# Four conv layers on one core: first loads and setup in steps, ln and exp in pieces, last sums ahead of the last products

## The chip, the cores and the metric

The kernel runs on one core of one Trainium2 chip. The core has a matmul engine (TensorE, PE in the profile, with its weight loads as PEld), a vector engine (VectorE, DVE), a scalar engine for activations (ScalarE, ACT), GpSimd (POOL) and a queue engine (SyncE, SP) that mostly issues DMAs. ACT and POOL issue DMAs too. SBUF is the on-chip memory of 128 partitions, PSUM the memory that PE writes. The metric is the device time in microseconds (us) of one execution, as the median of several runs.

## The reference, cut to what matters

Four layers act on x of shape (4, 64, 64, 64): four images of 4096 pixels with 64 channels, all float32.

```
# layer 0: attention over the pixels of each image
q = x @ Wq + bq ; k = x @ Wk + bk ; v = x @ Wv + bv
x = gamma * transposed_softmax_product(softmax(q k^T), v) + x   # einsum('bmn,bmc->bnc', attn, v)
# layer 1: a convolution block
y = pw1(layernorm(x)) ; y = depthwise3x3(y) ; y = y1 * y2 ; y = y * pw_sca(mean(y)) ; x = x + pw2(y) * beta
z = pw3(layernorm(x)) ; z = z1 * z2 ; x = x + pw4(z) * gamma
# layer 2: attention without weights, on x read as (B, C, H, W)
x = softmax(xf^T xf) applied to xf, + x
# layer 3: attention with 32 inner channels, then a normalisation over all images
f = softmax(theta(x) phi(x)^T) ; y = f g(x) ; w = y @ w_W + w_b
x = x + (gamma * (w - mean(w)) / sqrt(var(w) + 1e-3) + beta)     # mean and var over images and pixels
```

## The kernel before

**The work.** Each image's x lies in SBUF as `X[:, b]`: two halves of 64 partitions (the channels, for two groups of columns), 2048 numbers each. An attention layer is a loop over items. An item makes score tiles on PE into PSUM, ACT takes the exponential of each tile into an `e` buffer, and a later step multiplies these by the values, into an accumulator. PSUM has three score tiles of 1024 columns (`ps`, `new_ps`) and two accumulators of 512 (`acc`, `new_acc`); a new one takes over the oldest and waits until that is read. There are six `e` buffers and a ring of two `t` buffers (`new_t`), used in the same way.

**Layer 0** (L1018) has 32 items per image, each of four score tiles (L1031, exponential L1036), with products at L1056 that DVE adds up at L1063. `project0` (L971) makes the query and value projections of an image. For image 0 the queries come in four steps, with a bias add on DVE (L1002); for images 1 to 3 they come in two steps named "once" (L982), with two bias adds on DVE (L990) and a DMA on SP for each (L993) that copies the half to the other partitions. bq enters as `bqk`, a product of the folded weights with bq (`fold_qk`, L859 to 877).

**Layer 1** (L1112) is a generator of small steps, most of them on DVE (convolution taps L1157), some on PE and ACT, which runs under the items of layers 0 and 2. `setup` (L879) turns the small vectors of all layers into columns (`vec`), folds layer-norm scales and shifts into the weights `pw1` and `pw3` and their biases `pwb`, and builds the constants `half` and `resb`, which later steps use.

**Layer 2** (L1231) has 32 items per image, each of four score tiles (L1245, exponential L1253); products (L1262) come one item later. `close2` (L1289) scales and adds the result into x on DVE; `open3` (L1305) then makes theta, phi and g for layer 3 (L1315, L1325, L1340, with bias adds on DVE).

**Layer 3** (L1349) has two blocks of 32 items per image. An item makes two score tiles (L1361) and two exponentials (L1367) into one `e`; products (L1389) come two items later. The softmax's sums are collected in two ways: for every tenth item PE multiplies `e` by ones (L1378) into a second accumulator z; all others are added on DVE into `esum` (L1385), which `sums` (L1397) multiplies by ones at the block's end. When a block is done, ACT copies the product out (`yz`, L1395), `totals` (L1404) calls `sums`, takes 1/z as exp(-ln z) on ACT (L1410, L1411), improves it by a Newton step on DVE (L1412, L1413) and scales yz (L1414), and `close` (L1424) projects the block, adds a bias on ACT (L1432) and takes statistics on DVE. The last block of the last image ends in `close_last` (L1436).

**The order.** PE, ACT and DVE run in the order in which the program issues; a planner within the program sets it. `run` (L1495) first issues the start by hand: weights folded, half of image 0's x turned (`load_x`, L920), the query bias, the first query step, the second half of x. Then it goes through the items. After an item's scores, and again after the steps registered for that item by `at(i, fn)`, two lanes (`conv`, `misc`) tick by the item's number of microseconds; a generator in a lane runs its next step when the number that it last yielded has passed. So the numbers in `yield` are an order, not times. DMAs on SP, ACT and POOL go in the order of the program: x of image 0 is issued on SP and ACT (`fetch_x`, L738), then on SP bq, gamma, the small vectors (`rows`) and the x of images 1 to 3; the remaining weights are on POOL, behind the identity matrix.

**Layers in sequence**: layer 0 for images 0 to 3; layer 2 for image 0 and 1, layer 3 for image 0, layer 2 for image 2, layer 3 for image 1, layer 2 for image 3, layer 3 for images 2 and 3. So layer 2 of images 2 and 3 follows directly on a layer 3, and only layer 3 of image 3 follows on another layer 3.

**The end.** `finish` (L1536) combines the statistics and writes eight halves of images: three through PSUM (L1566, DVE L1585, stores L1575), five by an add on DVE (L1600), a turn on PE (L1607), a copy (L1627; L1630 and L1631 for the last), and a store of 512 KB (L1579). `check_sums` (L1635) counts values out of range into `bad`, which every engine reads before it ends.

Of the kernel before, what the change touches and what calls it, by code (L numbers as in the profile page):

```python
# [691 lines left out]
def fast_path(ctx: ExitStack, tc: tile.TileContext, a: dict, out: bass.AP, bad):  # L692
# [44 lines left out]

    def fetch_x(b, queues):  # L738
        if b % 2 == 0:
            fetch_x.both = new_big("xr")  # L740
        t = fetch_x.both[:, bass.ts(b % 2, 2048)].rearrange("p (q n) -> p q n", n=128)
        src = a["x"][b].rearrange(by_rows, p=2, q=16)
        for g in range(2):
            for p in range(2):
                (queues[p] if b == 0 else queues[g]).dma_start(
                    out=t[64 * p : 64 * p + 64, bass.ts(g, 8)], in_=src[p, :, bass.ts(g, 8)]
                )
        rows_x.append(t)
# [3 lines left out]
    nc.sync.dma_start(out=qk[:, 64:128], in_=a["L0_conv_Wk"])  # L752
    fetch_x(0, (nc.sync, nc.scalar))
    bq = const.tile([64, 1], F32, name="bq")
    nc.sync.dma_start(out=bq, in_=a["L0_conv_bq"].rearrange("(n o) -> n o", o=1))
# [123 lines left out]
    def setup():  # L879
# [7 lines left out]
        for i, (w_, sh, bi) in enumerate(  # L887
            ((pw1, "L1_conv_ln1_b", "L1_conv_pw1_b"), (pw3, "L1_conv_ln2_b", "L1_conv_pw3_b"))
        ):
            for r in range(2):  # L890
                mm(
                    ps[:, 2 * i + r : 2 * i + r + 1], w_[0:64, bass.ts(r, 128)], V(sh, 0, 0, 64),
                    start=True, stop=True,
                )
            nc.vector.tensor_add(
                pwb[:, i, :], ps[:, 2 * i : 2 * i + 2], vec[:, col[bi] : col[bi] + 2]
            )

        ps = new_ps()
        for i, (w_, g) in enumerate(((pw1, "L1_conv_ln1_g"), (pw3, "L1_conv_ln2_g"))):  # L900
            nc.vector.tensor_scalar_mul(w_, w_, V(g))
            mm(ps[:, 512 * i : 512 * i + 256], cmat, w_, start=True, stop=True)
            nc.vector.tensor_copy(w_, ps[:, 512 * i : 512 * i + 256])
        for i in range(4):
            nc.vector.tensor_scalar_mul(half[:, bass.ts(i, 64)], ident[:, 0:64], 0.5)
            stt(
                half[:, bass.ts(i, 64)], ident[:, 64:128], -0.5 if i > 1 else 0.5,
                half[:, bass.ts(i, 64)], ALU.mult, ALU.add,
            )
        nc.vector.tensor_mul(resb[:, 0:1], V("L1_conv_pw2_b"), V("L1_conv_beta"))  # L910
        nc.vector.tensor_mul(resb[:, 1:2], V("L1_conv_pw4_b"), V("L1_conv_gamma"))
        yield 3.0
# [7 lines left out]
    def load_x(b):  # L920
        for g in range(2):
            ps = new_ps()
            for i in range(8):
                nc.tensor.transpose(ps[:, bass.ts(i, 128)], rows_x[b][:, 8 * g + i, :], ident)
            (nc.vector.tensor_copy if g else nc.scalar.copy)(X[:, b, bass.ts(g, 1024)], ps)
            yield 3.0
# [44 lines left out]
    def project0(b):  # L971
# [5 lines left out]
        for j, w in once if b else ((0, "q"), (0, "v"), (1, "q"), (2, "q"), (1, "v"), (3, "q")):  # L977
            ps = new_ps()
            if w == "once":
# [7 lines left out]
                for o in range(2):  # L987
                    own, other = slice(64 * o, 64 * o + 64), slice(64 - 64 * o, 128 - 64 * o)
                    n = bass.ts(2 * j + o, 512)
                    nc.vector.tensor_scalar_add(  # L990
                        qs[own, :, n], ps[own, :].rearrange("p (s n) -> p s n", s=2), bqk[own, :]
# [25 lines left out]

    def layer0(b):  # L1018
# [3 lines left out]
        def scores(t):  # L1022
# [3 lines left out]
            for g in range(4):  # L1026
                ps = new_ps()
# [203 lines left out]
    def layer2(b):  # L1231
# [51 lines left out]
        for n in range(32):  # L1283
            items.append((lambda n=n: scores(n), 4.6))
            at(first + n + 1, lambda n=n: products(n))
# [3 lines left out]
    def close2(b):  # L1289
# [4 lines left out]
        for i in range(4):  # L1294
# [4 lines left out]
            yield 2.0 if i < 3 else 6.0  # L1299
# [3 lines left out]
    wys, early = {}, []  # L1303

# [44 lines left out]
    def layer3(b):  # L1349
# [3 lines left out]
        def scores(n):  # L1353
# [12 lines left out]
            for kp in range(2):  # L1366
                act(e[:, bass.ts(kp, 1024)], tiles[kp], AF.Exp)  # L1367

        def products(n):
# [4 lines left out]
            if mc % 10 == 9 or (last and n >= 62):  # L1374
# [9 lines left out]
            elif mc:  # L1384
                nc.vector.tensor_add(esum, esum, e)  # L1385
            if last and n == 63:
                sums()
            for k in range(4):
                mm(  # L1389
                    st["y"][32 * k : 32 * k + 32, :], m.gx[:, mc, :], e[:, bass.ts(k, 512)],  # L1390
                    start=mc == 0, stop=mc == 31,
                )
            if mc == 31 and not (last and n == 63):
                st["yz"] = new_t("yz")
                nc.scalar.copy(st["yz"][:, 0:512], st["y"])  # L1395

# [7 lines left out]
        def totals(nb):  # L1404
            sums()
            yz, z = st["yz"], st["z"]

            t = new_t("inv")
            r, d = t[:, 0:512], t[:, 512:1024]
            act(r, z, AF.Ln)  # L1410
            act(r, r, AF.Exp, scale=-1.0)  # L1411
            nc.vector.tensor_mul(d, z, r)  # L1412
            stt(d, d, -2.0, r, ALU.add, ALU.mult, accum_out=inv3[:, 2 * b + nb : 2 * b + nb + 1])  # L1413
            stt(yz[:, 0:512], d, -1.0, yz[:, 0:512], ALU.mult, ALU.mult)  # L1414

# [42 lines left out]
        for n in range(64):  # L1458
# [4 lines left out]
            elif n % 32 == 31:  # L1463
                at(first + n + (2 if n == 63 and b < 2 else 4), lambda n=n: totals(n // 32))
                at(first + n + 8, lambda n=n: close(n // 32))
# [29 lines left out]
    def run():  # L1495
# [6 lines left out]
        next(loads)  # L1502
        misc.add(first)
# [32 lines left out]
    def finish():  # L1536
# [34 lines left out]
        def store(i, o):  # L1571
            dst = out[i // 2].rearrange(by_rows, p=2, q=16)[:, :, bass.ts(i % 2, 8)]
            if i < E:
                for p in range(2):
                    nc.sync.dma_start(  # L1575
                        out=dst[p].rearrange("h q n -> h (q n)"), in_=o[64 * p : 64 * p + 64, 0:1024]
                    )
            else:
                nc.sync.dma_start(out=dst.rearrange("p h q n -> h p (q n)"), in_=o[:, 0:1024])  # L1579
# [42 lines left out]
        for i in range(E, 2 * B):  # L1622
# [5 lines left out]
            else:  # L1628
                check_sums(mv)
                nc.vector.tensor_copy(os[i][:, 0:512], pss[i][:, 0:512])  # L1630
                nc.scalar.copy(os[i][:, 512:1024], pss[i][:, 512:1024])  # L1631
            store(i, os[i])
# [74 lines left out]
```

## Time and profile before

| | |
|---|---|
| median of 3 runs | 2654.57 us (2653.53 to 2654.67) |
| profiled execution, its own time | 2654.59 us |
| its span, first to last instruction | 2652.8 us |
| PE, DVE, ACT, POOL busy | 2612.8, 1348.6, 1718.6, 16.4 us |
| mean granted PE clock | 0.997 |
| score matmul groups L1031, L1245, L1361 on PE | 475.5, 469.8, 309.5 us |
| product groups L1056, L1262, L1389 on PE | 467.4, 468.5, 272.0 us |
| exponentials L1036, L1253, L1367 on ACT | 517.1, 517.0, 496.0 us |
| esum adds L1385 on DVE, one | 2.29 us |

A line of the timeline gives the start and length of a group of instructions in us, engine, source line, operation, output and input, the count, and in brackets how long the engine was idle just before and what ended that. A line of waits gives the waiting engine and line, what it waited for, the total in us, how often, and the longest. A line of a table of windows gives the window, its length, the busy us and count of PE, PEld, DVE, ACT and POOL, the granted PE clock, the share of time in which the DMA engines were busy, and GB/s.

### The profile page before, as it was taken

The numbers are of one execution on the slowest core, as the hardware profiler recorded it, in microseconds if no ns is written. First come the engines' busy times: TensorE is split into PE (matmuls) and PEld (weight loads), VectorE is DVE, ScalarE is ACT, GpSimd is POOL, SyncE is SP. The second block draws the span as 40 slices with busy tenths as digits, with TensorE's granted clock in tenths as the row PEclk, the third lists the DMA queues.
The fourth block names the chain that finished last, engine by engine and source line by source line (L and its number), as shares of the span: only waits on it lengthen the run. The fifth ranks groups of instructions, "written<-read, shape, count | busy, mean of one in ns | idle before, by whom it ended". The sixth has DMA issues, their size and how long they took to land.

```text
span 2652.8 us, 50797 instructions
## 1 busy us (share of the span) xinstructions
PE 2612.8 (98%) x22421; PEld 830.2 (31%) x22421; DVE 1348.6 (51%) x1555; ACT 1718.6 (65%) x2787; POOL 16.4 (1%) x66
## 2 busy tenths in 40 slices
PE   8999999999999999999999999999999999999998
PEld 3333233333323323333333322243322333322223
DVE  3232386633876338621672148800068600098997
ACT  4555655656566565666656668756578755578886
POOL 2000000000000000000000000000000000000000
PEclk9999999999999999999999999999999999999999
DMA  3000000001000100010010000010000010010002
GB/s 73 1 17 1 17 8 10 1 17 25 9 1 1 32 17 1 1 33 17 1 33 17 17 1 1 2 33 1 17 1 2 1 33 1 1 33 2 1 1 66
DMA packets 24282, 36.46 MB, mean 14 GB/s; under 512 B 3725, under 2 KB 12150, under 8 KB 24054
## 3 DMA queue, kind: packets, MB, share of 16 engines
q1 hardware_dynamic: 23141, 32.03, 5.5%
q8 instruction: 178, 2.92, 0.5%
q0 software_dynamic: 672, 0.56, 0.1%
q10 hardware_dynamic: 240, 0.54, 0.1%
q14 instruction: 51, 0.41, 0.1%
HBM read 4.80 MB, written 4.19 MB: 3 GB/s over the span
## 4 chain that ended last, share of the span: by engine, by line
PE 93%; DVE 4%; ACT 2%; issue 0%; DMA 0%; SPq 0%; DVEq 0%; ACTq 0%
PE acc L1056 17%; PE acc L1262 17%; PE ps L1031 17%; PE ps L1245 16%; PE ps L1361 10%; PE acc L1389 8%; PE ps L1118 2%; DVE tg L1385 2%; PE accz L1378 1%; ACT e L1253 1%; PE ps L1209 1%; PE ps L1186 1%; PE ps L1088 1%; PE ps L1340 1%; PE ps L1007 0%
## 5 line engine op out<-in xcount | busy, mean ns | idle before, releaser
L1036 ACT ACTIVATE e<-ps 128x1024 f32<-128x1024 f32 x512 | 517.1, 1025 | 338.1 <-PE ps L1031 225.8
L1253 ACT ACTIVATE e<-ps 128x1024 f32<-128x1024 f32 x512 | 517.0, 1025 | 305.0 <-PE ps L1245 304.9
L1367 ACT ACTIVATE e<-ps 128x1024 f32<-128x1024 f32 x512 | 496.0, 1022 | 85.4 <-PE ps L1361 78.3
L1385 DVE TENSOR_TENSOR tg<-tg,e 128x2048 f32<-128x2048 f32 x214 | 490.4, 2292 | 24.7 <-ACT e L1367 5.7
L1031 PE MATMUL ps<-X,q 64*64 64x512 f32 x4096 | 475.5, 599 | 7.6 <-DVE q L990 4.1
L1245 PE MATMUL ps<-ko 64*64 64x512 f32 x4096 | 469.8, 591 | 2.2 <-ACT ko L1227 1.6
L1262 PE MATMUL acc<-e,X 64*64 64x512 f32 x4096 | 468.5, 591 | 2.6 <-DVE inv L1412 1.6
L1056 PE MATMUL acc<-e,vq 128*64 128x512 f32 x2048 | 467.4, 598 | 0.0
L1063 DVE SCALAR_TENSOR_TENSOR yv<-acc,gam,yv 128x512 f32<-128x512 f32 x224 | 167.8, 750 | 322.6 <-PE acc L1056 311.7
L1157 DVE SCALAR_TENSOR_TENSOR y<-pad,vec,y 128x1024 f32<-128x1024 f32 x240 | 308.1, 1284 | 8.1 <-ACT pad L1141 1.0
L1361 PE MATMUL ps<-tg,ph 32*64 32x512 f32 x4096 | 309.5, 613 | 1.4 <-DVE tg L1329 0.5
L1389 PE MATMUL acc<-e,tg 128*32 128x512 f32 x2048 | 272.0, 603 | 1.5 <-ACT yz L1395 1.5
L1245 PEld LDWEIGHTS ps<-ko 64*64 64x64 f32 x4096 | 157.7, 132 | 288.1 <-issue 195.4
L1262 PEld LDWEIGHTS acc<-e,X 64*64 64x64 f32 x4096 | 159.1, 133 | 278.7 <-issue 263.3
L1031 PEld LDWEIGHTS ps<-X,q 64*64 64x64 f32 x4096 | 143.2, 133 | 323.7 <-issue 224.8
L1056 PEld LDWEIGHTS acc<-e,vq 128*64 128x64 f32 x2048 | 136.0, 136 | 315.1 <-issue 294.4
L1270 DVE TENSOR_TENSOR ph<-ph,acc 128x512 f32<-128x512 f32 x16 | 11.0, 688 | 379.6 <-ACT ph L1269 379.6
L1361 PEld LDWEIGHTS ps<-tg,ph 32*64 32x64 f32 x4096 | 79.5, 129 | 218.7 <-issue 143.2
L1389 PEld LDWEIGHTS acc<-e,tg 128*32 128x32 f32 x2048 | 43.5, 108 | 202.3 <-issue 196.3
L1253 ACT ACTIVATION_READ_ACCUMULATOR e<-ps 128x1 f32 x512 | 106.1, 207 | 0.0
L1036 ACT ACTIVATION_READ_ACCUMULATOR e<-ps 128x1 f32 x512 | 106.0, 207 | 0.0
L1141 ACT ACTIVATE pad<-ps,pwb 128x512 f32<-128x512 f32 x64 | 44.6, 697 | 45.7 <-PE ps L1118 39.0
(193 smaller groups left out, 939.9 us busy)
## 6 DMA issues: line engine op xcount, KB each, us to landing
xn<-t SPq DMA_DIRECT2D x64, 128.0 KB
ph<-tg SPq DMA_DIRECT2D x64, 128.0 KB
ko<-ko SPq DMA_DIRECT2D x16, 256.0 KB
xr<-in_x_dram SPq DMA_DIRECT2D x14, 256.0 KB
q<-q SPq DMA_DIRECT2D x12, 256.0 KB
out_dram<-o SPq DMA_DIRECT2D x5, 512.0 KB
out_dram<-o SPq DMA_DIRECT2D x6, 256.0 KB
xr<-in_x_dram ACTq DMA_DIRECT2D x2, 256.0 KB
```

The lines of the kernel that those rows point to most:

```text
L1031: mm(ps[64 * c : 64 * c + 64, bass.ts(r, 512)], m.q[rows_, 128 * t + 64 * c : 128 * t + 64 * c + 64], x[rows_, bass.ts(g, 512)], start=Tru ...
L1036: act(es[g // 2][:, bass.ts(g % 2, 1024)], ps, AF.Exp, bias=SHIFT0, accum_out=zs[:, g : g + 1],)
L1056: mm(accs[g][64 * r : 64 * r + 64, :], vq, es[half][:, 1024 * g + 512 * r : 1024 * g + 512 * r + 512], start=t == 2 * p, stop=t == 2 * p + 1,)
L1063: stt((x if p == 15 else m.y)[:, cols], accs[g], gam0, (m.y if p else x)[:, cols], ALU.mult, ALU.add,)
L1157: stt(y1, win, wt, y1, ALU.mult, ALU.add)
L1245: mm(ps[64 * c : 64 * c + 64, bass.ts(r, 512)], m.ko[rows_, 128 * jb + 64 * c : 128 * jb + 64 * c + 64], m.ko[rows_, bass.ts(2 * ib + r, 5 ...
L1253: act(es[n, jb], ps, AF.Exp, bias=SHIFT2, accum_out=m.zs[:, jb, ib : ib + 1])
L1262: mm(acc[r][64 * c : 64 * c + 64, :], xw[rows_, jb, :], es[n, jb][rows_, bass.ts(c, 512)], start=jb == 0, stop=jb == 31,)
L1361: mm(tiles[kp][64 * c : 64 * c + 64, bass.ts(i, 512)], m.ph[rows_, 128 * mc + 64 * c : 128 * mc + 64 * c + 64], m.th[rows_, bass.ts(nb, 51 ...
L1367: act(e[:, bass.ts(kp, 1024)], tiles[kp], AF.Exp)
L1385: nc.vector.tensor_add(esum, esum, e)
L1389: mm(st["y"][32 * k : 32 * k + 32, :], m.gx[:, mc, :], e[:, bass.ts(k, 512)], start=mc == 0, stop=mc == 31,)
```

## The change

It has eight parts.

- The first loads: x of image 0 comes in three pieces for each of SP and ACT instead of two; `load_x` turns it in three steps, the last of which is issued between the second and the third score tile of item 0 (`between`). bq is loaded first, on POOL's queue.
- `setup` yields more often: the bias products and weight scaling, then the products with `cmat`, then the four blocks of `half` one by one.
- The query bias of images 1 to 3 is added by ACT instead of DVE.
- `close2` yields 9.0 instead of 6.0 after its last step, ahead of `open3`.
- In layer 2 of images 2 and 3 the products of item 0 are issued one item later, just before those of item 1.
- In layer 3 the second exponential of the item in which a finished block's `yz` is copied is held until after that copy. `ln` and `exp` are cut into four pieces of 256 columns. After the second block of images 0 and 1, where layer 2 of the next image follows, they are still issued at once; after the others they are issued over the items 5 to 8 after the block's end, `newton` with the last of them. `close` comes 11 items after the block's end instead of 8.
- In the last block `e` of item 60 is also summed by PE, and the sums are finished ahead of the products of the last two items.
- The last half image is copied and stored in two halves, and `check_sums` comes after them.

```diff
+    parts = ((0, 4), (4, 8), (8, 16)), ((0, 8), (8, 16))
+
     def fetch_x(b, queues):
...
-        for g in range(2):
+        for lo, hi in parts[b > 0]:
             for p in range(2):
-                (queues[p] if b == 0 else queues[g]).dma_start(
-                    out=t[64 * p : 64 * p + 64, bass.ts(g, 8)], in_=src[p, :, bass.ts(g, 8)]
-                )
+                queues[p].dma_start(out=t[64 * p : 64 * p + 64, lo:hi], in_=src[p, :, lo:hi])
...
+    bq = const.tile([64, 1], F32, name="bq")
+    nc.gpsimd.dma_start(out=bq, in_=a["L0_conv_bq"].rearrange("(n o) -> n o", o=1))
     fetch_x(0, (nc.sync, nc.scalar))
-    bq = const.tile([64, 1], F32, name="bq")
-    nc.sync.dma_start(out=bq, in_=a["L0_conv_bq"].rearrange("(n o) -> n o", o=1))
...
-        for i, (w_, sh, bi) in enumerate(
-            ((pw1, "L1_conv_ln1_b", "L1_conv_pw1_b"), (pw3, "L1_conv_ln2_b", "L1_conv_pw3_b"))
-        ):
+        for i, (w_, _, sh, bi) in enumerate(folds):
             for r in range(2):
                 mm(
                     ps[:, 2 * i + r : 2 * i + r + 1], w_[0:64, bass.ts(r, 128)], V(sh, 0, 0, 64),
                     start=True, stop=True,
                 )
+        for i, (_, _, _, bi) in enumerate(folds):
             nc.vector.tensor_add(
                 pwb[:, i, :], ps[:, 2 * i : 2 * i + 2], vec[:, col[bi] : col[bi] + 2]
             )
 
+        for w_, g, _, _ in folds:
+            nc.vector.tensor_scalar_mul(w_, w_, V(g))
+        yield 5.0
         ps = new_ps()
-        for i, (w_, g) in enumerate(((pw1, "L1_conv_ln1_g"), (pw3, "L1_conv_ln2_g"))):
-            nc.vector.tensor_scalar_mul(w_, w_, V(g))
+        for i, (w_, _, _, _) in enumerate(folds):
             mm(ps[:, 512 * i : 512 * i + 256], cmat, w_, start=True, stop=True)
+        for i, (w_, _, _, _) in enumerate(folds):
             nc.vector.tensor_copy(w_, ps[:, 512 * i : 512 * i + 256])
+        nc.vector.tensor_mul(resb[:, 0:1], V("L1_conv_pw2_b"), V("L1_conv_beta"))
+        nc.vector.tensor_mul(resb[:, 1:2], V("L1_conv_pw4_b"), V("L1_conv_gamma"))
+        yield 5.0
         for i in range(4):
             nc.vector.tensor_scalar_mul(half[:, bass.ts(i, 64)], ident[:, 0:64], 0.5)
...
-        yield 3.0
+            yield 4.0
...
-        for g in range(2):
-            ps = new_ps()
-            for i in range(8):
-                nc.tensor.transpose(ps[:, bass.ts(i, 128)], rows_x[b][:, 8 * g + i, :], ident)
-            (nc.vector.tensor_copy if g else nc.scalar.copy)(X[:, b, bass.ts(g, 1024)], ps)
+        for lo, hi in ((0, 8), (8, 16)) if b else parts[0]:
+            ps, n = new_ps(), 128 * (hi - lo)
+            for i in range(lo, hi):
+                nc.tensor.transpose(ps[:, bass.ts(i - lo, 128)], rows_x[b][:, i, :], ident)
+            (nc.vector.tensor_copy if lo == 8 else nc.scalar.copy)(
+                X[:, b, 128 * lo : 128 * hi], ps[:, 0:n]
+            )
             yield 3.0
...
-                    nc.vector.tensor_scalar_add(
-                        qs[own, :, n], ps[own, :].rearrange("p (s n) -> p s n", s=2), bqk[own, :]
+                    act(
+                        qs[own, :, n], ps[own, :].rearrange("p (s n) -> p s n", s=2),
+                        AF.Identity, bias=bqk[own, :],
                     )
...
+                if g == 2 and between:
+                    between.pop()()
                 ps = new_ps()
...
-            at(first + n + 1, lambda n=n: products(n))
+            at(first + n + (2 if n == 0 and b > 1 else 1), lambda n=n: products(n))
...
-            yield 2.0 if i < 3 else 6.0
+            yield 2.0 if i < 3 else 9.0
...
-            for kp in range(2):
-                act(e[:, bass.ts(kp, 1024)], tiles[kp], AF.Exp)
+            act(e[:, 0:1024], tiles[0], AF.Exp)
+            held.append(lambda: act(e[:, 1024:2048], tiles[1], AF.Exp))
+            if not (mc == 1 and (nb or last)):
+                held.pop()()
+            for fn in small.get(first + n, []):
+                fn()
...
-            if mc % 10 == 9 or (last and n >= 62):
+            if mc % 10 == 9 or (last and n >= 60):
...
+            if last and n == 62:
+                return
             if last and n == 63:
                 sums()
-            for k in range(4):
-                mm(
-                    st["y"][32 * k : 32 * k + 32, :], m.gx[:, mc, :], e[:, bass.ts(k, 512)],
-                    start=mc == 0, stop=mc == 31,
-                )
+            for i in (n - 1, n) if last and n == 63 else (n,):
+                for k in range(4):
+                    mm(
+                        st["y"][32 * k : 32 * k + 32, :], m.gx[:, i % 32, :], es[i][:, bass.ts(k, 512)],
+                        start=mc == 0, stop=i % 32 == 31,
+                    )
             if mc == 31 and not (last and n == 63):
                 st["yz"] = new_t("yz")
                 nc.scalar.copy(st["yz"][:, 0:512], st["y"])
+                if held:
+                    held.pop()()
...
+        def log(cols):
+            st["inv"] = st.get("inv") or new_t("inv")
+            act(st["inv"][:, cols], st["z"][:, cols], AF.Ln)
+
+        def exp(cols):
+            act(st["inv"][:, cols], st["inv"][:, cols], AF.Exp, scale=-1.0)
+
...
+        def totals(n):
+            sums()
+            steps = [
+                lambda: log(slice(0, 256)), lambda: log(slice(256, 512)),
+                lambda: exp(slice(0, 256)), lambda: exp(slice(256, 512)), lambda: newton(n // 32),
+            ]
+            for i, fn in enumerate(steps):
+                if n == 63 and b < 2:
+                    fn()
+                else:
+                    small.setdefault(first + n + 5 + min(i, 3), []).append(fn)
...
-                at(first + n + (2 if n == 63 and b < 2 else 4), lambda n=n: totals(n // 32))
-                at(first + n + 8, lambda n=n: close(n // 32))
+                at(first + n + (2 if n == 63 and b < 2 else 4), lambda n=n: totals(n))
+                at(first + n + 11, lambda n=n: close(n // 32))
...
         next(loads)
+        between.append(lambda: next(loads))
...
-            else:
-                check_sums(mv)
-                nc.vector.tensor_copy(os[i][:, 0:512], pss[i][:, 0:512])
-                nc.scalar.copy(os[i][:, 512:1024], pss[i][:, 512:1024])
-            store(i, os[i])
+                store(i, os[i])
+        i = 2 * B - 1
+        nc.vector.tensor_copy(os[i][:, 0:512], pss[i][:, 0:512])
+        store(i, os[i], 0)
+        nc.scalar.copy(os[i][:, 512:1024], pss[i][:, 512:1024])
+        store(i, os[i], 1)
+        check_sums(mv)
```

## The prediction

> **What bounds the kernel now.** I read the page first: the engines' shares and the chain of waits.
>
> ```profile
> PE 2612.8 (98%) x22421; PEld 830.2 (31%) x22421; DVE 1348.6 (51%) x1555; ACT 1718.6 (65%) x2787; POOL 16.4 (1%) x66
> PE 93%; DVE 4%; ACT 2%; issue 0%; DMA 0%; SPq 0%; DVEq 0%; ACTq 0%
> ```
>
> TensorE (PE) is busy for all but 40.0 us of a span of 2652.8. The change removes no large block of matmuls, so it can win only PE's idle time, stretches in which PE counts as busy but runs slowly, and the tail after the last product. So next I asked what PE waited for (total, times, longest):
>
> ```profile
> PE ps L1031 <- DVE q L990: 4.1, 2, 3.1
> PE ps L924 <- DMA xr<-in_x_dram: 2.1, 1, 2.1
> PE acc L1262 <- DVE inv L1412: 1.6, 2, 0.8
> PE acc L1389 <- ACT yz L1395: 1.5, 5, 0.3
> PE acc L875 <- DMA bq<-in_L_conv_bq_dram: 1.2, 1, 1.2
> PE ps L891 <- issue: 1.0, 1, 1.0
> PE ps L902 <- DVE pw L901: 0.8, 1, 0.8
> ```
>
> These are the places that the change touches. Then the timeline around each (start, length, engine and line, idle before). Setup and the item after it:
>
> ```profile
> 47.24 0.57 PE L891 MATMUL ps<-vec,pw 64*128 64x1 f32 x4 [0.98 <-issue]
> 48.39 0.67 PE L902 MATMUL ps<-pw,cmat 128*128 128x256 f32 x2 [0.57 <-issue]
> 49.84 0.81 PE L902 MATMUL ps<-pw,cmat 128*128 128x256 f32 x2 [0.78 <-DVE pw L901]
> 50.58 5.19 PE L1031 MATMUL ps<-X,q 64*64 64x512 f32 x32
> 55.70 3.65 PE L1056 MATMUL acc<-e,vq 128*64 128x512 f32 x16
> ```
>
> The 32 score matmuls take 5.19 us here and 3.66 elsewhere. The table of windows gives the granted clock (the column ahead of the last two):
>
> ```profile
> 51.00:52.00 1.00, 1.00 (x8) 0.24 (x4) 0.90 (x7) 0.00 (x0) 0.00 (x0) 0.50 0.03 8
> ```
>
> PE idled 2.33 us and then ran at half clock. The same follows image 2's query projection:
>
> ```profile
> 401.30 2.59 DVE L990 TENSOR_SCALAR q<-ps,bqk 64x1024 f32<-64x1024 f32 x2
> 403.95 1.09 PE L1031 MATMUL ps<-X,q 64*64 64x512 f32 x8 [3.15 <-DVE q L990]
> 406.31 3.17 PE L1007 MATMUL ps<-wv,X 128*128 128x128 f32 x16
> ```
>
> Here the bias add stands behind the convolution in VectorE's (DVE's) queue and holds a PSUM tile; L1007 x16 takes 3.17 instead of 2.05. The start of layer 2 for image 2 (image 3 is alike):
>
> ```profile
> 1711.60 1.07 PE L1262 MATMUL acc<-e,X 64*64 64x512 f32 x2 [0.30 <-ACT yz L1395]
> 1713.49 3.23 PE L1262 MATMUL acc<-e,X 64*64 64x512 f32 x27 [0.82 <-DVE inv L1412]
> ```
>
> And the end, where the DMA engines (column before the last) are full while every engine is done:
>
> ```profile
> 2646.00:2647.00 1.00, 0.00 (x0) 0.00 (x0) 0.00 (x0) 0.00 (x0) 0.00 (x0) 0.50 1.03 410
> ```
>
> **The change, part by part.**
>
> **A, the start: -1.2.** Before, PE waits for x until 6.93 and for bq until 10.10, makes q at 10.62 and starts scores at 14.43; item 0's scores end at 18.85. After: the first x piece is 256 KB of the 512 that landed by 6.93; the DMA rate row has about 905 KB moved by 6.75 and half of that by 4.85, so I estimate 5.0. Four transposes (half of L924's 1.94) to 6.0, the ScalarE (ACT) copy (0.59, L1395's row) to 6.7, q (1.99, as before) to 8.7, four more transposes to 9.7: scores start near 10. bq leaves SP, where it landed 7.1 us after its issue behind x, for the head of POOL's queue: its 0.57 us of issue delays ident's memset and select to about 2.0, before the 3.01 at which the weights land; wv and the other POOL loads slip 0.6, first used at 18.86. SP gives up bq and takes one x piece, so gam and the rows stay. ACT's extra x issue (0.62) moves its table load to about 3.3, done by 4.6, before the copy at 6.0. What is given back: the last eight transposes and DVE's copy (1.23) now stand between the second and the third score tile, and the third waits for the copy. Two tiles at half speed (1.8 each) to 13.6, or 13.2 if the clock rises on the way, transposes 1.0 to 14.2, copy to 15.5, two tiles to 17.4: -1.5. Before, the clock rises at about 16.4, where PE's matmuls per us double from 8 to 16, and the slow stretches last 3.4 us, so I count in such steps: 13.0 is one earlier. If it still comes only at 16.4, -0.3; if at 9.6, -3.1. I take -1.2, nearer the first, because 2.9 busy us ahead of 13.0 did not raise it before.
>
> **B, setup in steps: -3.9.** The same matmuls (0.60, 0.57, 0.67, 0.67) come in two runs without a DVE result awaited between them: bias sums end at 46.8, scores(4) at 50.4, the cmat products at 51.7, where L1056 started at 55.70. That is 2.33 idle and 1.53 of slow clock. DVE scales the weights under scores(4) (3.6 us against 0.7); without that cover the 0.78 stays. The half blocks and resb go into DVE gaps of 2 to 5 us per item.
>
> The **Trainium skill** ("TensorE: Matmul & The Clock Gate", part 1) puts the half clock after at least one idle window of some 3.4 us, free-running against the kernel. Here 2.33 us of idle in pieces sufficed, so the row decides. By the rule the slow clock would not be due to these gaps and 1.5 stays: 2641.5 instead of 2640.0.
>
> **C, query bias on ACT: -5.1.** Image 2: 0.42 + 3.15 idle, and the slow clock: L1118's start to L1007's is 1.45 instead of 1.02, L1007 lasts 3.10 instead of 1.98, together 1.55. ACT has been idle for 6.79 us there; two biases of about 1.14 (L1432's Identity) run from 397.2 to 399.5, so the third score tile waits 0.4: -4.7. Image 1: -0.4 (0.23 idle, 0.2 stretch). Image 3's stall of 0.98: ACT has a 1.42 us pad step in front at 663.1, ends the biases at 666.6, where DVE ended too: 0. Behind each bias on ACT wait the next exponentials, and PE for their tiles; at up to 5 us of work per 7.2 us item ACT catches up. The SP copies of q start earlier, and the norm's broadcasts behind them too. The skill's "ScalarE: Activation LUTs" (rules for kernel authors) says adds belong on VectorE, which is faster. The rows say 1.29 for DVE and 1.14 for ACT in f32; by the rule C gives only what the queue gives, less a slower add: at double the time 2.3 more stall in each of images 2 and 3, 2644.6.
>
> **D, close2's longer pause: -0.4.** Only layer 3 of image 2 can feel it: five items take 18.2 us for 5 x 2.12 + 5.7 of open3's matmuls, 1.9 lost. The pause lets X finish, but the theta and phi adds stay behind DVE's 2.29 us sums. Between 0 and -1.9; nearer 0.
>
> **E, layer 2's first product one item later: -3.3.** From the end of sums at 1711.3 to the second product group at 1720.14 is 8.83 for 7.18 of matmuls: 1.65 lost, twice. After: scores(2) run at 1711.3; all three PSUM tiles are free by 1711.0 (ACT's last exponential), ACT's copy, ln and exp pieces end at 1713.0, so the fourth tile is free at 1714.05, when PE comes to it. The six e buffers just hold: the last two belong to layer 3's sums, done at 1708.9.
>
> **F, layer 3's block ends (five): 0.** Steady items take 2.12 us with ACT idle 0.16 to 0.21. From the start of the item with the yz copy, 11 items (through sums, close and the first ones-product) take 26.75. The held exponential, itself now behind PE's last y product, takes PE's 0.31 wait away, but ACT's 0.59 copy still goes in, and PE meets it as a late PSUM tile: 0 to -0.3. Before, ln and exp (1.24) run while PE does sums (0.9): 0.25 lost. In four items, each piece of 0.35 exceeds the idle 0.18: +0.7. Back comes 0.3 at the close, where ACT stood 0.76 behind L1383, itself behind newton. Newton (2.1 us on DVE) now waits for the last exp with DVE idle some 3.7 us, and the esum adds behind it run up to 5.6 late; the e buffers come free about 3.6 us before ACT needs them, so nothing. Net +0.1 each, between -0.5 and +0.8; I take 0.
>
> **G, last sums: -0.3.** n=60 gets ones-products (+0.86 PE) and DVE loses a 2.29 sum, so the 0.37 wait at L1399 goes; ln starts at 20.35 instead of 21.13 (2600 left out), but the first projection still follows begin_out, 0.2 later, the second at 24.7 instead of 25.09. +0.2 to -0.6.
>
> **H, store in halves: -0.4.** The last issue moves from 2644.86 to about 2644.6, and check_sums (2.2 us) goes under the DMA tail: `bad` at 2645.6, SP's branch by 2648, and SP waits for landings until 2651.1. But 1.33 MB are still to move at 2645.6 at 400 GB/s: the queue is the bound. 0 to -1.0; nearer 0.
>
> Sum: -1.2 - 3.9 - 5.1 - 0.4 - 3.3 + 0 - 0.3 - 0.4 = -14.6. The profiled execution took 2654.59, its span 2652.8 and 1.8 around it; the median of the runs is 2654.57, so **2640.0** stands for both.
>
> **Rivals.**
>
> *The clock keeps dipping elsewhere* (3.1 us): for it, the gate's phase is not the kernel's; against it, both dips follow the stalls that go. 2643.1.
>
> *ACT becomes the wait at the projections*: C gives 1 instead of 5.1, if the biases queue behind pad steps as for image 3. Against it the 6.79 us of idle at image 2. 2644.1.
>
> *The pieces at layer 3 cost their full 0.8*: ACT idles only 0.18 per item. 5 x 0.8: 2644.0.
>
> *The start and the tail give all*: clock one window earlier (-1.9 more), last store -0.6 more, close2 -1: 2636.5.
>
> *Slower*: newton's wait on DVE is not covered. The adds 5.6 us late hold e buffers, ACT's exponentials stop, PE follows: 5 x 5.6 = 28, 2668. It decides once a block end loses over 2.9 us; the 3.6 us margin speaks against it.
>
> **How the numbers follow.** Forecast 0.50 (2637.5 to 2643), clock 0.11, ACT at projections 0.11, pieces 0.11, all of start and tail 0.13, slower 0.04. The range 2634.5 to 2645.5 takes in all but the last and the outer ends of the bounds (all low 2631, all high 2648). A measurement tells 0.2% (5.3 us) from no change: faster is below 2649.3. Faster 0.95, same 0.02, slower 0.03.
>
> **What would show it.** A: scores start near 10. B and C: full clock at 50 to 54 and 405 to 409, and no wait on L990's successor above 0.5. E: no wait of layer 2's first products. F: five stretches of 11 items at 26.3 to 27.6; ACT waiting on L1385 there would be the slower rival. G and H: under 1 us between them. Wrong would be a new slow window, or block ends losing over 1 us each.

## The result and the profile after

The changed kernel takes **2637.28 us** (median of 4 runs, 2636.40 to 2637.78), beside 2654.05 for the kernel before on the same chip (4 runs, 2653.16 to 2654.67). The ratio is 0.9937, with a 95% interval of 0.9919 to 0.9954: 16.8 us faster, where the prediction had 14.6. The profiled execution took 2637.78, its span is 2635.8. The page's busy shares and chain of waits:

```profile
PE 2607.8 (99%) x22429; PEld 821.6 (31%) x22429; DVE 1331.1 (51%) x1542; ACT 1730.5 (66%) x2814; POOL 17.1 (1%) x67
PE 97%; ACT 1%; DVE 1%; issue 0%; DMA 0%; SPq 0%; ACTq 0%
```

PE is now idle for 28.0 us (2635.8 less 2607.8) instead of 40.0, and counts 5.0 us less as busy: for the most part those are the slow stretches. Its remaining waits, of those that bear on the change (total, times, longest):

```profile
PE acc L1699 <- DVE inside L1697: 2.3, 1, 2.3
PE ps L1045 <- ACT q L999: 1.7, 2, 1.0
PE ps L1045 <- DVE X L932: 1.4, 1, 1.4
PE ps L931 <- DMA xr<-in_x_dram: 0.7, 1, 0.7
PE acc L1276 <- DVE X L1077: 0.3, 1, 0.3
```

The 4.1 behind the query bias is 1.7 now and stands behind ACT. The waits for bq and for layer 2's products are gone; a new one, 1.4, stands behind the copy of x's third piece. The first line is in the tail, where the range checks now come last. Setup, in the timeline of PE:

```profile
41.06 3.65 PE L1070 MATMUL acc<-e,vq 128*64 128x512 f32 x16
44.64 1.05 PE L893 MATMUL ps<-vec,pw 64*128 64x1 f32 x8
45.62 3.66 PE L1045 MATMUL ps<-X,q 64*64 64x512 f32 x32
49.22 1.13 PE L907 MATMUL ps<-pw,cmat 128*128 128x256 f32 x4
50.28 3.65 PE L1070 MATMUL acc<-e,vq 128*64 128x512 f32 x16
```

No idle time, and 3.66 for the 32 scores that took 5.19. The same at image 2's projection, and ACT's side of it:

```profile
391.29 1.90 PE L1045 MATMUL ps<-X,q 64*64 64x512 f32 x16
393.84 1.09 PE L1045 MATMUL ps<-X,q 64*64 64x512 f32 x8 [0.65 <-ACT q L999]
395.10 1.09 PE L1045 MATMUL ps<-X,q 64*64 64x512 f32 x8 [0.17 <-ACT e L1050]
396.10 1.09 PE L1132 MATMUL ps<-xn,pw 64*64 64x512 f32 x8
397.12 2.05 PE L1017 MATMUL ps<-wv,X 128*128 128x128 f32 x16
...
391.54 2.25 ACT L999 ACTIVATE q<-ps,bqk 64x1024 f32<-64x1024 f32 x2 [3.77 <-PE ps L991]
```

L1017 x16 takes 2.05 where it took 3.17. The record of the granted clock has no dip at either place: it is full from 13.10 to 2627.71, which is behind the last products. The start of layer 2 for image 2:

```profile
1700.20 1.04 PE L1424 MATMUL accz<-tg,ones 128*32 128x512 f32 x8
1701.17 3.66 PE L1259 MATMUL ps<-ko 64*64 64x512 f32 x32
1704.66 7.05 PE L1276 MATMUL acc<-e,X 64*64 64x512 f32 x64
1711.52 3.61 PE L1259 MATMUL ps<-ko 64*64 64x512 f32 x32
```

Scores first, then both product groups, and nothing waits. The tail ends as before, with full DMA engines (windows; the column before the last) and idle engines:

```profile
2629.00:2630.00 1.00, 0.00 (x0) 0.00 (x0) 0.00 (x0) 0.00 (x0) 0.00 (x0) 0.50 1.01 412
```

**Where the time went.** Every layer-0, 2 and 3 exponential has a counterpart in the other trace: 1536 of them, in the same order. The difference of their start times, after less before, is a running account of the gain:

| place | offset, us | step since the row above |
|---|---|---|
| image 0, item 1 | -1.01 | A, the start |
| image 0, item 5 | -5.42 | B, setup: -4.4 |
| image 1, item 12 | -6.10 | C, image 1's projection: -0.7 |
| image 1, item 18 | -10.30 | C, image 2's: -4.2 |
| image 2, item 18 | -9.71 | C, image 3's: +0.6 |
| layer 3 of image 0, item 43 | -10.15 | D -0.16, F -0.28 |
| layer 2 of image 2, item 11 | -12.47 | E (with a little of D): -2.3 |
| layer 3 of image 1, item 43 | -12.75 | F: -0.3 |
| layer 2 of image 3, item 11 | -15.07 | E (with a little of D): -2.3 |
| layer 3 of image 2, item 20 | -16.15 | D: -1.1 |
| layer 3 of image 3, item 43 | -16.79 | F: -0.26, -0.19, -0.19 |
| the scaled identity behind the statistics | -17.19 | G: -0.4 |
| end of the span | -17.1 | H: +0.1 |

An experiment is read in the same account, against after. Item 1 serves as its zero, because the start scatters: the eight runs below whose code is unchanged up to there put item 1 between 0.09 us later and 1.57 us earlier than after's 22.70. A single time of one run therefore says less than its account; all runs but 8 are one execution each.

### The profile page after: what moved, and what is told of

It reads as the page before. It is cut to its first block, busy times and chain, and to the rows that moved or that the text cites. A ratio compares the mean times of both kernels' runs of the same rounds, so it can differ in the third digit from the quotient of the medians.

```text
span 2635.8 us, 50835 instructions
## 1 busy us (share of the span) xinstructions
PE 2607.8 (99%) x22429; PEld 821.6 (31%) x22429; DVE 1331.1 (51%) x1542; ACT 1730.5 (66%) x2814; POOL 17.1 (1%) x67
## 4 chain that ended last, share of the span: by engine, by line
PE 97%; ACT 1%; DVE 1%; issue 0%; DMA 0%; SPq 0%; ACTq 0%
PE acc L1070 17%; PE ps L1045 17%; PE acc L1276 17%; PE ps L1259 16%; PE ps L1377 11%; PE acc L1412 10%; PE ps L1132 2%; PE accz L1398 1%; PE ps L1017 1%; PE ps L1223 1%; PE ps L1200 1%; PE ps L1102 1%; PE ps L1356 1%; PE ps L931 0%; ACT e L1267 0%; PE ps L1289 0%
## 5 line engine op out<-in xcount | busy, mean ns | idle before, releaser
L1050 ACT ACTIVATE e<-ps 128x1024 f32<-128x1024 f32 x512 | 517.0, 1025 | 310.9 <-PE ps L1045 211.4
L1267 ACT ACTIVATE e<-ps 128x1024 f32<-128x1024 f32 x512 | 517.1, 1025 | 302.3 <-PE ps L1259 302.2
L1382 ACT ACTIVATE e<-ps 128x1024 f32<-128x1024 f32 x256 | 262.8, 1027 | 84.4 <-PE ps L1377 70.3
L1383 ACT ACTIVATE e<-ps 128x1024 f32<-128x1024 f32 x256 | 261.4, 1021 | 0.0
```

Of the source, the lines that this page charges most:

```text
L1050: act(es[g // 2][:, bass.ts(g % 2, 1024)], ps, AF.Exp, bias=SHIFT0, accum_out=zs[:, g : g + 1],)
L1267: act(es[n, jb], ps, AF.Exp, bias=SHIFT2, accum_out=m.zs[:, jb, ib : ib + 1])
L1382: act(e[:, 0:1024], tiles[0], AF.Exp)
L1383: held.append(lambda: act(e[:, 1024:2048], tiles[1], AF.Exp))
```

## The experiments

**1. Setup back in two steps (B undone).**

```diff
-        for w_, g, _, _ in folds:
-            nc.vector.tensor_scalar_mul(w_, w_, V(g))
-        yield 5.0
         ps = new_ps()
-        for i, (w_, _, _, _) in enumerate(folds):
+        for i, (w_, g) in enumerate(((pw1, "L1_conv_ln1_g"), (pw3, "L1_conv_ln2_g"))):
+            nc.vector.tensor_scalar_mul(w_, w_, V(g))
             mm(ps[:, 512 * i : 512 * i + 256], cmat, w_, start=True, stop=True)
-        for i, (w_, _, _, _) in enumerate(folds):
             nc.vector.tensor_copy(w_, ps[:, 512 * i : 512 * i + 256])
...
```

The bias sums, too, are each added at once again, and `half` and `resb` come in one step.

> The changed kernel with setup put back into two steps, all else as changed. Theory (the ledger: each edit is worth what it saves at its own place, and the slow clock at 50 us was caused by the gaps in setup): PE idles about 2.3 us again at 46 to 50 us, a slow stretch of 3.4 us follows it, and all exponentials after item 5 come 4.0 to 4.4 us later than in the changed kernel; time near 2641.5. Rival (the clock drops by the phase of its own window, not for these gaps): the gaps return without the slow stretch, 2.3 to 2.8 us later, time near 2640.

Measured: 2640.88. The account goes from -1.57 at the start to +2.83 from item 10 on: **+4.4**, just what the two traces had given. PE's timeline in this run:

```profile
44.65 0.57 PE L891 MATMUL ps<-vec,pw 64*128 64x1 f32 x4 [0.98 <-issue]
45.80 0.67 PE L902 MATMUL ps<-pw,cmat 128*128 128x256 f32 x2 [0.57 <-issue]
47.25 0.87 PE L902 MATMUL ps<-pw,cmat 128*128 128x256 f32 x2 [0.78 <-DVE pw L901]
48.05 5.13 PE L1038 MATMUL ps<-X,q 64*64 64x512 f32 x32
```

and its windows, with the granted clock in the third column from the end:

```profile
48.00:49.00 1.00, 1.00 (x9) 0.35 (x12) 0.81 (x4) 0.00 (x0) 0.00 (x0) 0.50 0.00 0
50.00:51.00 1.00, 1.00 (x12) 0.30 (x8) 0.17 (x3) 0.90 (x1) 0.00 (x0) 0.50 0.00 0
51.00:52.00 1.00, 1.00 (x12) 0.29 (x8) 0.00 (x0) 0.68 (x3) 0.00 (x0) 0.97 0.00 0
```

The three gaps return with the very lengths that they had before, and the half clock with them, although this place comes 2.5 us earlier here. This is where the prediction chose the row over the rule of the Trainium skill ("TensorE: Matmul & The Clock Gate", part 1). The rule's length of idle time does not hold here: 2.33 us in three pieces, less than its whole idle window, bring 3.41 us of half clock in both traces that have them, and without them it does not come. Its free-running window does show, in steps of 3.41 us in the clock's record (last section). Whether such gaps bring the half clock also depends on how they lie in these steps.

**2. The query bias back on DVE (C undone).**

```diff
-                    act(
-                        qs[own, :, n], ps[own, :].rearrange("p (s n) -> p s n", s=2),
-                        AF.Identity, bias=bqk[own, :],
+                    nc.vector.tensor_scalar_add(
+                        qs[own, :, n], ps[own, :].rearrange("p (s n) -> p s n", s=2), bqk[own, :]
                     )
```

> The changed kernel with the query bias of images 1 to 3 added by DVE again. Theory: image 2's second projection waits again behind the convolution (3 to 4 us of PE idle near 394 us) with a slow stretch after it, image 3's stall gets 0.2 to 0.6 shorter; exponentials at the end of layer 0 come 4.0 to 4.5 us later, time near 2641.5. Rival (ACT only took the wait over, and the gain at 400 us came from a shift between the convolution's steps and the projection in time): without the shift that edits A and B made, the stall comes out differently, and the difference is under 2 us.

Measured: 2641.02. In the account, image 1 gives +0.6, image 2 +4.0, image 3 **-0.6**: +4.0 in all. PE's timeline, and a window of it:

```profile
397.36 1.99 PE L1044 MATMUL ps<-X,q 64*64 64x512 f32 x8 [3.14 <-DVE q L999]
399.12 1.54 PE L1131 MATMUL ps<-xn,pw 64*64 64x512 f32 x8
```
```profile
398.00:399.00 1.00, 1.00 (x8) 0.25 (x4) 0.00 (x0) 0.00 (x0) 0.00 (x0) 0.50 0.99 209
```

Wait and half clock are both back. The rival, that ACT merely becomes the wait in DVE's place, falls for image 2; for image 3 it is right, and the edit loses 0.6 us there.

**3. Layer 2's first products one item after their scores (E undone).**

```diff
-            at(first + n + (2 if n == 0 and b > 1 else 1), lambda n=n: products(n))
+            at(first + n + 1, lambda n=n: products(n))
```

> The changed kernel with layer 2's first products of images 2 and 3 one item after their scores again. Ledger from the two traces: 2.3 us lost in each image, 4.6 in all, time near 2642. The prediction's own sum, with layer 0's 3.59 us for a group of 32 matmuls: 1.65 each, 3.3, time near 2640.6. With layer 2's own period of 6.87 us per item in that sum it is 2.0 each.

Measured: 2642.10; the account has +2.24 at image 2's layer 2 and +2.27 at image 3's, 4.5 together and nothing elsewhere. The gain is E's alone, and larger than forecast.

**4 and 7. Layer 3's block ends: ln and exp whole, and the close (F).** Run 4 undoes all of F: the second exponential is not held, ln and exp are issued whole behind `sums`, and `close` comes after 8 items. Run 7 keeps the hold and the close after 11 items, and only issues ln, exp and Newton's step as before, whole and at once.

```diff
-            for i, fn in enumerate(steps):
-                if n == 63 and b < 2:
-                    fn()
-                else:
-                    small.setdefault(first + n + 5 + min(i, 3), []).append(fn)
+            if n < 63 or b > 1:
+                steps = [lambda: log(slice(0, 512)), lambda: exp(slice(0, 512)), steps[4]]
+            for fn in steps:
+                fn()
...
-            if not (mc == 1 and (nb or last)):
-                held.pop()()
+            held.pop()()                                    # run 4 only
...
-                at(first + n + 11, lambda n=n: close(n // 32))
+                at(first + n + 8, lambda n=n: close(n // 32))   # run 4 only
```

> The changed kernel with layer 3's block ends as before: nothing held, ln and exp whole and at once after the sums, newton at once, close at 8 items. The prediction's F: no difference (between 0.8 faster and 0.5 slower for each of five ends, sum 0). Ledger from the two traces: 0.2 to 0.4 us later for each of five ends, 1.4 in all, time near 2638.7.

> The changed kernel with ln and exp whole, at once after the sums, newton at once; the held exponential and the close at 11 items stay. It parts F: if the pieces are what gains, each of five block ends is 0.2 to 0.4 us later than in the changed kernel; if the gain is the later close, the ends are within 0.1; by the prediction's count of 0.18 us lost per piece, each end would be 0.3 to 0.5 faster.

Measured: run 4 takes 2639.42, and its account rises by 1.2, from -0.14 to 1.07; at the block ends by 0.2 each. Run 7 takes 2637.64; over each of the five ends its account moves by 0.1 or less, and mostly downwards. Both accounts rise by 0.3 besides between layer 2 of image 2 and item 20 of layer 3 of image 1, where no block ends; the cause of that loss is open. So the pieces bring nothing at the ends; what F gains there is the hold and the later close, which no run separates. The traces do not settle it. With the hold, PE's wait of 0.30 us for `yz` (before and run 4) is gone, but in run 7 the next score group takes 1.67 us instead of run 4's 1.11. ACT waited 0.76 us before for DVE's L1383, queued behind Newton's step, and 0.75 in run 4; in run 7 and in after it does not. But the wait stands ahead of the close, whose matmuls (L1419) start at 1645.62 before. In the timelines of ACT, before and then after:

```profile
1639.06 3.82 ACT L1367 ACTIVATE e<-ps 128x1024 f32<-128x1024 f32 x4
1643.63 3.78 ACT L1367 ACTIVATE e<-ps 128x1024 f32<-128x1024 f32 x4 [0.76 <-DVE tg L1383]
```
```profile
1639.82 1.03 ACT L1382 ACTIVATE e<-ps 128x1024 f32<-128x1024 f32 x1 [0.18 <-PE ps L1377]
1640.74 1.02 ACT L1383 ACTIVATE e<-ps 128x1024 f32<-128x1024 f32 x1
1641.95 1.02 ACT L1382 ACTIVATE e<-ps 128x1024 f32<-128x1024 f32 x1 [0.19 <-PE ps L1377]
```

**5. bq behind x (the early bq of A undone, x still in three pieces).**

```diff
-    bq = const.tile([64, 1], F32, name="bq")
-    nc.gpsimd.dma_start(out=bq, in_=a["L0_conv_bq"].rearrange("(n o) -> n o", o=1))
     fetch_x(0, (nc.sync, nc.scalar))
+    bq = const.tile([64, 1], F32, name="bq")
+    nc.sync.dma_start(out=bq, in_=a["L0_conv_bq"].rearrange("(n o) -> n o", o=1))
```

> The changed kernel with bq loaded on SP behind x again, as before; x still in three pieces. Theory: bq then lands near 10 us as before, its product stands between the first transposes and the query on PE, so PE waits from 6.4 to about 10.1, the query is made at 10.7 instead of 7.2 and scores start near 13.6 instead of 10.2; item 1 comes 2 to 3.5 us later, or less where the clock rises earlier against it. Rival: the smaller x pieces alone bring the early start, bq was hidden; then item 1 moves by under 0.5.

Measured: 2639.96; item 1 at 24.97, against 22.70 for after and 23.71 for before. PE's timeline:

```profile
5.43 1.09 PE L931 MATMUL ps<-ident,xr 128*128 128x128 f32 x4 [0.72 <-DMA rows<-in_L_conv_pw_b_dram]
10.07 0.58 PE L875 MATMUL acc<-bq,qkt 64*128 64x1 f32 x2 [3.55 <-DMA bq<-in_L_conv_bq_dram]
10.58 1.99 PE L1007 MATMUL ps<-X,wq 64*64 64x512 f32 x8
```

bq, 256 bytes issued at 3.58, has landed by 10.03, behind x. That is 2.3 us lost on after, more than the start's scatter, and 1.3 on before's one trace, which is within it: without the early bq, x in pieces shows no gain. The step depends on where 256 bytes stand in a queue.

**6 and 10. The tail (H).** Run 6 keeps the store in halves and moves the range checks ahead of the last two copies. Run 10 undoes H: checks first, and one store behind both copies.

```diff
+        check_sums(mv)
         nc.vector.tensor_copy(os[i][:, 0:512], pss[i][:, 0:512])
-        store(i, os[i], 0)                                  # run 10 only
         nc.scalar.copy(os[i][:, 512:1024], pss[i][:, 512:1024])
-        store(i, os[i], 1)                                  # run 10: store(i, os[i])
-        check_sums(mv)
```

> The changed kernel with the range checks ahead of the last copies again; the last store still in halves. The prediction's H said that checks under the DMA tail cost nothing, so that putting them back can only lose (0 to 1.0 us later at the end, from the last store issued later). Rival from the trace: every engine branches over the other path only after it has read the result of the checks, and the first instructions after the branch come 4.6 us later; with checks last the branch and the last store end together, so putting the checks first gives 0 to 0.5 us between the last copy of the statistics and the end.

> The last store is whole again, behind both copies, with the range checks ahead of them: step H undone alone. The prediction's H (0.4 gained, the DMA queue the bound): about +0.4, 2637.7. The theory from the two traces (H lost 0.2, the end is set by the last landing plus a fixed remainder): -0.2 to 0, 2637.1. From the last projection product to the end of the span after took its own time; that distance is what is to be compared, since the start scatters by 1.4.

Measured: 2637.77 and 2637.40. From the last exponential to the end of the span, run 6 takes as long as after and run 10 0.1 less. H gains nothing. In after, the second half's issue begins on SP at 2628.09 and takes 1.16, since the first half's issue, 1.16 as well, stands ahead of it; in run 10 the whole store is issued at 2627.84 in 0.33.

**9. The pause in layer 2's close (D undone).**

```diff
-            yield 2.0 if i < 3 else 9.0
+            yield 2.0 if i < 3 else 6.0
```

> The pause at the end of layer 2's last shift is 6.0 again, all else as after: step D undone alone. Counted on the exponentials, D is the offset against after that appears between image 2's layer 3 near item 10 and its item 20. The theory (the pause gives what the ledger of the two traces shows there, 15.07 to 15.99): +0.9, about 2638.2. The rival, my forecast of nearer 0 (0.4): +0.4 or less, and the rest of the 0.9 came from the block end of step F. No effect at all would show under 0.1.

Measured: 2638.1, from a start at -1.32. The account gains 0.17, 0.15 and 0.17 in layer 2 of images 1, 2 and 3, and +1.08 in layer 3 of image 2, where PE's timeline shows both of the adds that the longer pause lets pass:

```profile
2339.07 1.12 PE L1377 MATMUL ps<-tg,ph 32*64 32x512 f32 x16 [0.48 <-DVE tg L1335]
...
2344.86 1.12 PE L1377 MATMUL ps<-tg,ph 32*64 32x512 f32 x16 [0.49 <-DVE tg L1345]
```

In after, theta (L1331) and phi (L1341) come one to two items later, at 2338.71 and 2344.80 instead of 2334.63 and 2341.11, and no tile waits. D is worth 1.1 there and 1.6 in all.

**8. Three mends.** What the two accounts show as lost or idle: the third piece of x is turned between the first and second score tile instead of the second and third, so that DVE's copy runs under a tile; image 3's bias goes back to DVE; and the range checks run as soon as their inputs are there, two of them in `close_last`.

```diff
-                if g == 2 and between:
+                if g == 1 and between:
...
-                    act(
-                        qs[own, :, n], ps[own, :].rearrange("p (s n) -> p s n", s=2),
-                        AF.Identity, bias=bqk[own, :],
-                    )
+                    if b < 3:                       # as above, on ACT
+                        ...
+                    else:                           # image 3: nc.vector.tensor_scalar_add(...)
+                        ...
...
         def close_last():
+            check(0, sums0.rearrange("p b t -> p (b t)"), LO, HI)
+            check(1, sums2.rearrange("p b t -> p (b t)"), LO, HI)
```

The other two checks follow the statistics, and the count stands ahead of the last stores.

> The changed kernel with three mends: the last piece of image 0's x is turned between the first and the second score tile instead of the second and the third; image 3's query bias is back on DVE; the range checks of the sums run in close_last, where DVE idles, and the rest before the last stores. Theory: PE's 1.41 us wait for DVE's copy of x goes (item 1 comes 1.2 to 1.4 earlier), image 3's projection gives 0.5 and the end 0 to 0.5: 1.7 to 2.4 us in all, 2635.3. Rival: the third piece of x has not landed or ACT's copies take the wait over at the start, and nothing is gained there: 0.5 to 1.0.

Measured: **2634.54** (5 runs, 2634.36 to 2635.01), a ratio of 0.9926 to before, with an interval of 0.9912 to 0.9939: the best of all, and below every run of after, though the interval overlaps that of after. PE's timeline at the start:

```profile
9.94 1.33 PE L1050 MATMUL ps<-X,q 64*64 64x512 f32 x8
11.21 1.09 PE L931 MATMUL ps<-ident,xr 128*128 128x128 f32 x8
12.23 1.09 PE L1050 MATMUL ps<-X,q 64*64 64x512 f32 x8
13.71 1.95 PE L1050 MATMUL ps<-X,q 64*64 64x512 f32 x16 [0.39 <-DVE X L932]
```

The wait of 1.41 is 0.39 (1.0 us of the 2.26 by which item 1 is earlier; run 9, whose clock comes up at 10.52 against 10.49 here, has item 1 at 21.38 against 20.44). Image 3 gives the 0.6 back. From the last exponential to the end another 0.5 goes, with `bad` ready at 2622.53 instead of 2628.69; run 6 had moved it by 1.9 to no effect.

## Why the prediction was right

| step | forecast | account | undone alone |
|---|---|---|---|
| A, start | -1.2 | -1.0 | not as a whole; without the early bq +2.3 |
| B, setup | -3.9 | -4.4 | 4.4 |
| C, query bias | -5.1 | -4.3 | 4.0 |
| D, pause | -0.4 | -1.2 | 1.6 |
| E, first products | -3.3 | -4.6 | 4.5 |
| F, block ends | 0 | -1.2 | 1.2 |
| G, last sums | -0.3 | -0.4 | not tried |
| H, store in halves | -0.4 | +0.1 | -0.1 (faster) |
| sum (before rounding) | -14.6 | -17.1 | |

The time lies inside the range, 2.7 us below the forecast. Each of the three large terms is there, for the reason given. D, E and F gave 3.3 us more than forecast and B 0.5; A, C and H gave 1.5 less. The outer bounds of 2631 and 2648 do not come out of the terms, whose low ends add up to 2633.2 and whose high ends to 2646.2.

**A.** The chain held: first piece at 5.43 (estimate 5.0), scores at 10.15 ("near 10"), PE behind the copy of the third piece for 1.41. The size could not be called better than by its bounds: other runs with the same start put item 1 up to 1.6 us earlier, as their clock came up earlier (last section). That -1.0 lies so near the forecast is in part luck. With bq behind x (run 5) nothing is left of the step, which the prediction did not say.

**B.** Right, with the half clock where the gaps put it; the rest of 0.5 is that eight matmuls in one run take 1.05, where two runs of four took 0.60 and 0.57, and four take 1.13 instead of 0.67 and 0.81. The prediction added the old lengths.

**C.** The mechanism was right, and a size was off: two biases take 2.25 us on ACT, as forecast, but behind them the third score tile waits 0.65 and the fourth 0.17 more, not 0.4, and at image 3, which I set to 0, 1.03 and 0.17, more than the 0.98 that they replaced. The rule of the Trainium skill ("ScalarE: Activation LUTs", rules for kernel authors) that adds belong on DVE was weighed and not followed. Its order of speed, given for bf16, does not show here, in f32 from PSUM: two biases took 2.59 us on DVE and 2.25 on ACT. At image 2 DVE's queue and not its speed held the tile; at image 3, where no queue stood in the way, DVE gave 0.6 back (run 8).

**D.** Too small. The sentence that the theta and phi adds "stay behind DVE's 2.29 us sums" was the wrong step: with the pause they fall into places where nothing waits for them. -1.9 was the bound that I gave, and 1.6 was measured.

**E.** The mechanism was right; the term mis-sized is the cost of the matmuls to be taken off the 8.83. I put 7.18 there, the length of a layer-0 item, while layer 2's own item takes 6.87: in after, the two product groups run from 1704.66 to 1711.52. That is 0.3 of what is missing in each of the two; the account's 2.3 also holds 0.17 of D (run 9), and of run 3's 2.2 some 0.3 stay open.

**F.** "Each piece of 0.35 exceeds the idle 0.18: +0.7" failed, and run 7 shows it: two exponentials issued back to back start 0.92 apart and need some 1.84, so that a piece fits into an item of 2.12, and items with a piece take 2.09 to 2.16. The 0.25 "lost" to ln and exp before falls with it, since whole ones cost no more. What is left of my terms, the hold's 0 to -0.3 and the close's -0.3, makes -0.3 to -0.6 per end, and -0.2 to -0.3 was measured. Which of the two it is stays open: the 0.76 that I put at the close stands ahead of it (runs 4 and 7).

**H.** "The queue is the bound" fits, and by it the value was 0, the near end of the bounds that I gave, where I took -0.4. What failed is the issue time: the second half's issue was put at 2644.6, 0.3 earlier than the whole store's, and in after it ends later than that of run 10's whole store (2629.25 against 2628.17, with starts 0.4 apart).

**The rivals.** The clock does not dip elsewhere: it is full from 13.10 to the tail. ACT as the wait at the projections takes the whole gain at image 3 alone. The pieces cost nothing. The start and the tail did not give more. The slower case, Newton's wait on DVE, did not come: DVE waited 0.99 us for the last exp, and ACT never for an e buffer.

## What to carry to other kernels

On a chip where PE's clock follows its own gaps, cost a stall with what it does to the work behind it: gaps of 2.33 us in setup, with the half clock behind them and the groups that they cut up, cost 4.4. Take the price of a group from the stage in which it will run, since an item of four score tiles with its products takes 7.18 us in layer 0 here and 6.87 in layer 2. And before a step is put down to its name, undo its parts one at a time: the pieces of ln and exp were neutral, and the gain of the block ends came from what was moved beside them.

## What the runs showed of the hardware

- **Half clock after broken idle time.** Each trace holds a record of the clock's changes, finer than the windows. Up to the tail its stretches are whole multiples of 3.41 us: 34.13, 3.41 and 351.57 in before, for example. I cut all twelve traces into steps of 3.41 us from the first change on, some 9200 steps, and counted PE's idle time in each, one-column matmuls (such as L893's) as idle. Half clock followed every step at full clock with 2.00 us or more and none with 1.79 or less. At setup it was 2.28 in before and 2.34 in run 1; at image 2's projection 2.08 in before and 2.51 in run 2. That such small matmuls count as idle is an inference: with them as busy, setup has 1.71 and 1.77, and a step of 1.79 in run 5's tail brought no half clock. Shifting the steps over the setup of these two traces, I estimate that 2.00 us are reached at five of six positions, so a run with these gaps could also escape.
- **The start's clock.** In the first 15 us the same 16 score matmuls took 3.39 us in after and 1.98 in run 1, with the same code up to there. The windows show 1.00 for both because the record has no entry ahead of the first change, the rise to full clock: at 13.10 in after, 10.10 in run 1 and 16.16 in before. In the nine traces with after's start it lies between 10.10 and 13.29, and item 1 follows it in the same order, from 21.12 to 22.79. The spread, 3.2 us, is about one step of 3.41: the start's scatter fits where the steps happen to lie.
- **A jump at the end.** The engines read `bad` and jump over a branch that is not taken up. PE's branch in after begins at 2629.59 and lasts 4.59 us, in run 6 it begins at 2628.00 and lasts 5.51, in run 10 5.23 from 2627.44; run 8's, at 2623.98, lasts 4.85. An earlier `bad` is in part lost in a longer jump, and in part in the wait for the last store. That the jump is slowed by the stores is a guess; no run separates the two.
- **Shapes in turn.** Layer 0 alternates 128*64 products with 64*64 scores and takes 7.18 us per item; layer 2 has 64*64 for both and takes 6.87. At 128 items that is 40 us, more than twice what this change gave. Whether the shapes are the cause is not shown, as it wasn't tried.
